# The second layer of a two-layer convolution kernel, written as a pipeline over half images

## The chip, the cores and the metric

The kernel runs on one core of a Trainium2 chip. The time is the device time of one execution of the whole program in microseconds (us), median over runs. The core has a matrix engine (TensorE, PE in the profile), VectorE (DVE), ScalarE (ACT), GpSimd (POOL) and SyncE (SP), which here only issues transfers (DMA). The engines run their own instruction streams and wait for one another through semaphores. ScalarE issues transfers too, from the same stream as its arithmetic: a transfer that waits there holds up the arithmetic behind it.

## The reference, cut to what matters

The input x is 32 images of 8 channels of 256 x 256, fp32. Each of two layers normalises x by groups of channels (`_gn`) and adds a function of the result to x. Layer 0 (a 15-step lattice, two small networks and a gate) is the greater part of the work and isn't touched. Layer 1 is a quantised 3 x 3 convolution:

```python
def _quantize(v, scale):
    return jnp.clip(jnp.round(v * scale), -MAX_Q, MAX_Q)
sx = MAX_Q / jnp.max(jnp.abs(x))          # over all 32 images
sw = MAX_Q / jnp.max(jnp.abs(weight))
qx = _quantize(x, sx)
qw = _quantize(weight, sw)
out_i32 = lax.conv_general_dilated(qx, qw, ...)   # 8 -> 8 channels, 3 x 3, padding 1
out = out_i32 / (sx * sw)
return out + bias[None, :, None, None]
...
x = x + _L1_conv_ref(_gn(x), L1_conv_weight, L1_conv_bias)
```

MAX_Q is 127. `sx` needs the largest value of all images, so layer 1 can't begin for any image before layer 0 has ended for all.

## The kernel before, in words

Layer 0 leaves its result y in HBM (`y_s`, one buffer per image, rows of 8 channels x 256 columns, with zero rows around them), and per image a mean `mean_y`, a factor `rstd_y` and a largest deviation `dev_y`. From line 898 on, layer 1 takes one image after the other.

An image is cut into 19 bands (`NB`) that step by 14 rows (`STEP`). Partition p of a band holds row p // 8 and channel p % 8, so 128 partitions are 16 rows of 8 channels: 14 output rows and a row of margin on each side. A tile of y is thus 128 x 19 x 256 fp32. The last band has 4 rows of output.

First come loads for three images, the largest deviation over partitions (a GpSimd all-reduce, L919) and small scale vectors (L921 to L929): `qs` has the scale, and two copies of it that zero the margin rows outside the image, for the first and the last band. Then, for each image b:

- VectorE subtracts the mean and scales, y to `tq` (L940 to L943, three instructions: band 0, bands 1 to 17, band 18).
- VectorE rounds `tq` to whole numbers in place, by adding and subtracting 1.5 x 2^23 (L944).
- VectorE clips to -127 and 127 and converts to bf16, `tq` to `qt` (L946). `qt` has a zero column on either side; there are two, taken in turn.
- TensorE runs over two bands at a time (512 columns), three matmuls for the three columns of the kernel, summed in a PSUM bank (L953). The rows and the channels are in the 128 x 128 weights `qw`.
- ScalarE scales each bank back, adds the bias and writes it to the output tile `ob` (L954); 10 such evictions make an image.
- ScalarE's queue issues the load of image b + 3 (L909), VectorE adds y to `ob` (L957), and SyncE issues 19 stores, one for each band, of 112 partitions x 1 KB (the last 32 partitions) to `out` (L960).

There are two `ob` tiles, four of y, one `tq` and four PSUM banks. An `ob` tile is free when all 19 stores have landed. The order on each engine around these lines is set by a scheduler, which takes the program's order as a priority and its own costs: ScalarE's queue issues the loads in pairs, and VectorE's sum of one image and scaling of the next change places in some images. Every transfer signals its landing on one of eight semaphores, taken in turn, and a transfer waits for the earlier one on the same semaphore, so that no more than eight are under way.

Of the kernel before, what the change touches and what calls it, by code (L numbers as in the profile page):

```python
# [31 lines left out]
F32 = mybir.dt.float32  # L32
BF16 = mybir.dt.bfloat16
F32R = mybir.dt.float32r
AF = mybir.ActivationFunctionType
ALU = mybir.AluOpType
AX = mybir.AxisListType
DRAM = bass.MemoryType.DRAM
PSUM = bass.MemoryType.PSUM

P = 128
C = 8
# [4 lines left out]
MAX_Q = 127.0  # L47
ROUND = 1.5 * 2.0**23

NB = 19  # L50
STEP = 14
PW = W + 2
# [61 lines left out]
def kernel(  # L114
# [15 lines left out]
    nc = tc.nc  # L130
    B = x.shape[0]
    V, S, G, T = nc.vector, nc.scalar, nc.gpsimd, nc.tensor

    def dram_ap(t, offset, dims):
        return bass.AP(t.tensor, t.offset + offset, dims)
# [17 lines left out]
    qw = cp.tile([P, 3, P], BF16, name="qw")  # L153
# [6 lines left out]
    mean_y = cp.tile([P, B], F32, name="mean_y")  # L160
# [96 lines left out]
    with ExitStack() as one:  # L257

        one.enter_context(tc.manual_schedule(engines={mybir.EngineType.PE}))
        pool = lambda name, bufs, **kw: one.enter_context(tc.tile_pool(name=name, bufs=bufs, **kw))  # L260
# [115 lines left out]
        def lattice(g):  # L376
# [77 lines left out]
            if g == 0:  # L454
                units[0], dmas = load(0)
                for d in dmas:
                    nc.sync.dma_start(*d)
                for ts in tiles:
                    begin(units[0], ts)
            for c in range(C):  # L460
                u = g * C + c
                ds = units[u]
                for step in range(STEPS):
                    if step == 7 and u + 1 < NG * C:
                        units[u + 1], dmas = load(u + 1)
                        later.extend(dmas)
# [363 lines left out]
        def chain(*gens):  # L830
            for gen in gens:
                yield from gen
# [15 lines left out]
        def both(a, t_a, b, t_b):  # L848

            done_a = done_b = 0.0  # L850
            while a or b:
                if b is None or a and done_a * t_b <= done_b * t_a:
                    w = next(a, None)
                    if w is None:
                        a = None
                        continue
                    done_a += w
                else:
                    w = next(b, None)
                    if w is None:  # L860
                        b = None
                        continue
                    done_b += w
                yield w

        def prep(g, halves):
            return normalise([(b, half) for half in halves for b in range(g * GB, g * GB + GB)])

        def images(f, g):
            for b in range(g * GB, g * GB + GB):  # L870
                yield from f(b)
# [3 lines left out]
        def after(g, gen):  # L875

            while issued[0] < stored[g]:
                yield 4.0
            yield from gen
# [3 lines left out]
        for g in range(NG):  # L883
            fill, t = images(nca, g), T_NCA
            if g:
                fill, t = both(fill, t, after(g - 1, images(gate, g - 1)), T_GATE), t + T_GATE
            if g + 1 < NG:
                fill, t = both(fill, t, prep(g + 1, (0, 1)), T_PREP), t + T_PREP
            if g == 0:
                fill, t = chain(prep(0, (1,)), fill), t + 20.0  # L890
# [7 lines left out]
    with ExitStack() as two:  # L898


        pool = lambda name, bufs, **kw: two.enter_context(
            tc.tile_pool(name=name, bufs=bufs, reuse_waits="tile", **kw)
        )
        tp, qp, op, sp, yp = pool("tp", 1), pool("qp", 2), pool("op", 2), pool("sp", 1), pool("yp", 4)
        ps = pool("ps", 4, space=PSUM)

        def load(b):
            y = yp.tile([P, NB, W], F32, name="yb", tag="yb")
            (nc.sync if b < 3 else nc.scalar).dma_start(  # L909
                y, dram_ap(y_s[b], 0, [[W, P], [STEP * C * W, NB], [1, W]])  # L910
            )
            return y

        ys = {b: load(b) for b in range(3)}

        gmax = sp.tile([P, 1], F32, name="gmax")
        V.tensor_reduce(gmax, dev_y, AX.X, ALU.max)
        gall = sp.tile([P, 1], F32, name="gall")
        G.partition_all_reduce(gall, gmax, P, bass.bass_isa.ReduceOp.max)  # L919
        sx = sp.tile([P, 1], F32, name="sx")  # L920
        V.reciprocal(sx, gall)  # L921
        V.tensor_scalar(sx, sx, MAX_Q, None, ALU.mult)
        inv = sp.tile([P, 1], F32, name="inv")
        V.tensor_tensor(inv, sx, sw, ALU.mult)
        V.reciprocal(inv, inv)
        qs = sp.tile([P, 3, B], F32, name="qs")
        V.tensor_scalar(qs[:, 0, :], rstd_y, sx, None, ALU.mult)
        V.tensor_scalar(qs[:, 1, :], qs[:, 0, :], masks[:, 2:3], None, ALU.mult)
        V.tensor_scalar(qs[:, 2, :], qs[:, 0, :], masks[:, 3:4], None, ALU.mult)  # L929
        qt = [qp.tile([P, NB, PW], BF16, name=f"qt{i}", tag=f"qt{i}", bufs=1) for i in range(2)]  # L930
        for t in qt:
            V.memset(t[:, :, 0], 0.0)
            V.memset(t[:, :, PW - 1], 0.0)

        for b in range(B):
            y = ys.pop(b)

            t = tp.tile([P, NB, W], F32, name="tq", tag="tq")
            for k0, k1, i in ((0, 1, 1), (1, NB - 1, 0), (NB - 1, NB, 2)):
                V.tensor_scalar(  # L940
                    t[:, k0:k1, :], y[:, k0:k1, :], mean_y[:, b : b + 1], qs[:, i, b : b + 1],
                    ALU.subtract, ALU.mult,
                )  # L943
            V.tensor_scalar(t, t, ROUND, ROUND, ALU.add, ALU.subtract)  # L944
            q = qt[b % 2]
            V.tensor_scalar(q[:, :, 1 : 1 + W], t, MAX_Q, -MAX_Q, ALU.min, ALU.max)  # L946
            o = op.tile([P, NB, W], F32, name="ob", tag="ob")
            for p in range(10):
                k0, n = 2 * p, (2 if p < 9 else 1)
                pt = ps.tile([P, 512], F32, name="pt2", tag="pt2")  # L950
                pt = pt[:, : n * W].rearrange("p (k w) -> p k w", w=W)
                for dx in range(3):
                    T.matmul(pt, qw[:, dx, :], q[:, k0 : k0 + n, dx : dx + W], start=(dx == 0), stop=(dx == 2))  # L953
                S.activation(o[:, k0 : k0 + n, :], pt, AF.Identity, bias=bv[:, 3:4], scale=inv)  # L954
            if b + 3 < B:
                ys[b + 3] = load(b + 3)
            V.tensor_tensor(o, o, y, ALU.add)  # L957
            for k in range(NB):
                rows = STEP if k < NB - 1 else 4
                nc.sync.dma_start(  # L960
                    dram_ap(out, b * C * H * W + STEP * k * W, [[W, rows], [H * W, C], [1, W]]),
                    o[C : C + rows * C, k, :],
                )


# [43 lines left out]
```

## Time and profile before

The time is 14360.28 us, the median of 3 runs (14354.44 to 14362.28). The profiled execution took 14414.7 us.

| what | value |
|---|---|
| span of the profiled execution | 14414.7 us |
| layer 0, up to the first load of y for layer 1 | 13636.3 us |
| layer 1, from there to the end | 778 us |
| 13700 to 14380 us: TensorE, VectorE, ScalarE, GpSimd busy | 244, 467, 199, 0 of 680 us |
| same: DMA engines' mean share, rate | 0.62, 189 GB/s |
| one load of y, one store of a band | 2432 KB, 112 KB |

Lines of the page with L940 to L960 belong to layer 1. In a row of a group, the numbers after `|` are busy us, mean ns of one instruction, the idle time just before the group's instructions and what ended most of it. In a row of waits, they are us in total, times, longest. In a table of stretches, each engine has busy us and the number of instructions, and the last three columns are the granted clock of TensorE as a share of the full one, the mean busy share of the 16 DMA engines and the rate. "ACTq" and "SPq" are the transfers that ScalarE and SyncE issue; the time that such a row gives is the issuing alone, not the transfer.

### The profile page before, as it was taken

How to read it: one execution, taken by the hardware profiler on the slowest of the kernel's cores; microseconds unless marked ns; L12 is line 12 of the kernel's file. 1: busy time of each engine (PE TensorE's matmuls, PEld its weight loads, DVE VectorE, ACT ScalarE, POOL GpSimd, SP SyncE). 2: the span in 40 equal slices, each digit the busy share in tenths (PEclk: the TensorE clock that was granted, in tenths of full speed). 3: DMA queues.
4: the chain of work that ended last, by engine and by line, in shares of the span. 5: the costliest groups of instructions: out<-in, count | busy, mean ns of one | idle time of the engine just before them, and what ended most of it. 6: DMA issues, size and time to landing. Idle time of an engine off the chain costs nothing.

```text
span 14414.7 us, 229163 instructions
## 1 busy us (share of the span) xinstructions
PE 13267.4 (92%) x81728; PEld 6423.3 (45%) x81728; DVE 8213.1 (57%) x16290; ACT 4039.8 (28%) x6274; POOL 2445.9 (17%) x4266
## 2 busy tenths in 40 slices
PE   2999999999999999999999999999999999999833
PEld 1554444444444444444444444444444444444311
DVE  3555555555555555555555555555555555555576
ACT  1333232232222222222322223222323222222122
POOL 1111111111111111111111111111111111112300
PEclk9999999999999999999999999999999999999966
DMA  5444444444444444444444434444444433333465
GB/s 148 93 97 92 90 103 106 103 94 100 110 94 100 99 106 94 103 100 95 100 103 107 98 93 106 110 94 94 104 104 98 103 88 88 80 83 78 122 195 176
DMA packets 2259559, 1496.74 MB, mean 104 GB/s; under 512 B 1061248, under 2 KB 2229504, under 8 KB 2258304
## 3 DMA queue, kind: packets, MB, share of 16 engines
q1 hardware_dynamic: 2176976, 1401.95, 41.9%
q10 hardware_dynamic: 81456, 80.12, 1.7%
q8 instruction: 664, 10.88, 0.3%
q14 instruction: 463, 3.79, 0.1%
HBM read 866.48 MB, written 478.69 MB: 93 GB/s over the span
## 4 chain that ended last, share of the span: by engine, by line
PE 70%; DMA 9%; DVE 9%; SPq 5%; issue 3%; POOL 2%; ACT 1%; ACTq 1%; POOLq 0%; DVEq 0%
PE pt L487 31%; PE ph L567 18%; PE pa L759 13%; PE acc L584 7%; DVE gt L495 2%; DMA im<-xp_s 1%; PE pg L725 1%; DMA xp_s<-lo 1%; SPq L545 1%; DVE m_b L500 1%; DMA xb<-in_x_dram 1%; DMA m_a<-m_a 1%; DMA out_dram<-ob 1%; SPq L960 1%; PE pt L953 1%
## 5 line engine op out<-in xcount | busy, mean ns | idle before, releaser
L487 PE MATMUL pt<-m_a,lw 128*64 128x390 f32 x17280 | 5827.0, 497 | 186.4 <-DMA m_a<-m_a 122.4
L487 PE MATMUL pt<-m_b,lw 128*64 128x384 f32 x17280 | 5796.6, 492 | 19.2 <-DVE m_b L410 18.0
L577 ACT ACTIVATE h<-ph,bp_sb 128x512 f32<-128x512 f32 x4096 | 2584.6, 684 | 6491.5 <-PE ph L567 6423.0
L487 PEld LDWEIGHTS pt<-m_a,lw 128*64 128x64 f32 x17280 | 2298.4, 138 | 1884.0 <-issue 1681.2
L487 PEld LDWEIGHTS pt<-m_b,lw 128*64 128x64 f32 x17280 | 2306.6, 138 | 1560.0 <-issue 1423.6
L567 PE MATMUL ph<-im,wp_hi 48*128 48x512 f32 x12288 | 2800.2, 419 | 174.2 <-DVE gt L495 113.1
L567 PE MATMUL ph<-im,wp_lo 48*128 48x512 f32 x12288 | 2675.2, 402 | 0.0
L495 DVE SCALAR_TENSOR_TENSOR gt<-pt,d_b 128x390 f32<-128x390 f32 x2880 | 1605.3, 557 | 1714.7 <-PE pt L487 1711.2
L495 DVE SCALAR_TENSOR_TENSOR gt<-pt,d_a 128x384 f32<-128x384 f32 x2880 | 1580.3, 549 | 1694.5 <-PE pt L487 1694.1
L504 POOL TENSOR_TENSOR m_b<-m_b,junk 128x12 f32<-128x12 f32 x2688 | 795.5, 296 | 8193.8 <-DVE m_b L500 7517.2
L567 PEld LDWEIGHTS ph<-im,wp_hi 48*128 48x128 f32 x12288 | 1417.5, 189 | 1081.7 <-DVE gt L495 303.9
L500 DVE SCALAR_TENSOR_TENSOR m_b<-gt 128x390 f32<-128x390 f32 x2688 | 1546.1, 575 | 44.5 <-DVE gt L495 2.3
L500 DVE SCALAR_TENSOR_TENSOR m_a<-gt 128x384 f32<-128x384 f32 x2688 | 1522.3, 566 | 17.2
L567 PEld LDWEIGHTS ph<-im,wp_lo 48*128 48x128 f32 x12288 | 1417.0, 189 | 217.3
L584 PE MATMUL acc<-h,wu_z 128*32 128x512 f32 x8320 | 1165.6, 603 | 6.1 <-ACT nca L602 5.5
L759 PE MATMUL pa<-xnb,gw 128*64 128x512 f32 (+1 forms) x3840 | 879.9, 588 | 43.7 <-DVE xnb L700 43.5
L759 PE MATMUL pa<-cmb,gw 128*64 128x512 f32 (+1 forms) x3840 | 857.6, 577 | 17.4 <-POOL cmb L681 17.4
L759 PE MATMUL pa<-nb,gw 128*64 128x512 f32 (+1 forms) x3840 | 863.6, 576 | 0.0
L730 POOL TENSOR_TENSOR d<-cmb,nb 128x512 f32<-128x512 f32 x320 | 502.9, 1572 | 1460.6 <-DVE gate L734 1028.5
L700 DVE TENSOR_SCALAR xnb<-xb,sc 128x256 f32<-128x256 f32 x608 | 290.7, 493 | 796.7 <-DMA xb<-in_x_dram 759.5
L953 PE MATMUL pt<-qt,qw 128*128 128x512 bf16 (+1 forms) x960 | 269.5, 451 | 477.0 <-ACT ob L954 425.4
L734 DVE TENSOR_TENSOR gate<-gate,d 128x512 f32<-128x512 f32 x320 | 217.4, 679 | 764.7 <-ACT gate L727 756.7
(132 smaller groups left out, 6928.0 us busy)
## 6 DMA issues: line engine op xcount, KB each, us to landing
im<-xp_s SPq DMA_DIRECT2D x1152, 193.5 KB
im<-xp_s SPq DMA_DIRECT2D x1216, 96.8 KB
d_a<-xq_s SPq DMA_DIRECT2D x2048, 36.0 KB
nb<-nc_s SPq DMA_DIRECT2D x288, 256.0 KB
cq<-cm_s SPq DMA_DIRECT2D x288, 256.0 KB
yb<-y_s ACTq DMA_DIRECT2D x29, 2432.0 KB
xb<-in_x_dram SPq DMA_DIRECT2D x544, 128.0 KB
xp_s<-hi SPq DMA_DIRECT2D x256, 258.0 KB
```

Of the source, the lines that this page charges most:

```text
L487: T.matmul(pt[half], lw[:, c, k, half], beside if part == 2 else own, start=part < 2, stop=part > 0,)
L495: V.scalar_tensor_tensor(gt, pt, FLOOR, d[:, ts, :], ALU.max, ALU.add)
L500: V.scalar_tensor_tensor(to, gt, 1.0, gt, ALU.subtract, ALU.mult)
L504: G.tensor_tensor(edge, edge, junk.unsqueeze(1).to_broadcast([P, 6, 2]), ALU.mult)
L567: T.matmul(ph[:, :n].rearrange("p (h w) -> p h w", w=W), w[64 * i : 64 * i + 48, dx, :], rhs[:, :, dx : dx + W], start=(dx == 0 and w is w ...
L577: S.activation(h[:, :n], ph[:, :n], AF.Relu, bias=bp_sb)
L584: T.matmul(acc[32 * g : 32 * g + 32, :cols], wu_z[:, 24 - 8 * i : 56 - 8 * i], h, start=first, stop=last,)
L700: V.tensor_scalar(xnb[:, k, 1 : 1 + W], xb[:, k, :], sc[:, i : i + 1], sc[:, 1:2], ALU.subtract, ALU.mult,)
L730: G.tensor_tensor(three(d), cmb[:, :n, 1 : 1 + W], nin, ALU.subtract)
L734: V.tensor_tensor(y[:, :cols], gt[:, :cols], d[:, :cols], ALU.mult)
L759: T.matmul(three[half], gw[:, s * 3 + dx, half], t[:, :n, dx : dx + W], start=(i == 0), stop=(i == 8),)
L953: T.matmul(pt, qw[:, dx, :], q[:, k0 : k0 + n, dx : dx + W], start=(dx == 0), stop=(dx == 2))
```

## The change

Layer 1 is written as a software pipeline whose order on all engines is that of the program (`manual_schedule`), with an image cut into halves of 10 and 9 bands. In iteration b VectorE scales image b in halves (`scaled`), rounding together with the lower clip: the rounding constant is added, then max with the constant minus 127. GpSimd does the rest (`quantised`): min with the constant plus 127, subtract the constant, convert to bf16. VectorE then adds y to the output of image b - 1, SyncE issues its first 13 stores, TensorE and ScalarE convolve image b and evict it, and behind these evictions ScalarE issues the other 6 stores of image b - 1 and the load of image b + 3. The zero columns are written by GpSimd, the first four loads are all on SyncE, and there are 8 PSUM banks, four `ob` and two `tq` tiles of half an image each. It is for having the engines work on different images at once, taking a pass from VectorE, and sharing the stores between two queues.

```diff
+        two.enter_context(tc.manual_schedule())
...
-        tp, qp, op, sp, yp = pool("tp", 1), pool("qp", 2), pool("op", 2), pool("sp", 1), pool("yp", 4)
-        ps = pool("ps", 4, space=PSUM)
+        tp, qp, op, sp, yp = pool("tp", 2), pool("qp", 1), pool("op", 4), pool("sp", 1), pool("yp", 4)
+        ps = pool("ps", 8, space=PSUM)
...
-            (nc.sync if b < 3 else nc.scalar).dma_start(
+            (nc.sync if b < 4 else nc.scalar).dma_start(
...
+        qt = [[qp.tile([P, n, PW], BF16, name=f"qt{i}{j}") for j, n in enumerate((10, 9))] for i in range(2)]
+        for t in (*qt[0], *qt[1]):
+            G.memset(t[:, :, 0], 0.0)
+            G.memset(t[:, :, PW - 1], 0.0)
+        HALVES = ((0, 10), (10, NB))
+        def scaled(b, y, h):
+            h0, h1 = HALVES[h]
+            t = tp.tile([P, 10, W], F32, name="tq", tag="tq")
             for k0, k1, i in ((0, 1, 1), (1, NB - 1, 0), (NB - 1, NB, 2)):
...
-            V.tensor_scalar(t, t, ROUND, ROUND, ALU.add, ALU.subtract)
-            q = qt[b % 2]
-            V.tensor_scalar(q[:, :, 1 : 1 + W], t, MAX_Q, -MAX_Q, ALU.min, ALU.max)
+            V.tensor_scalar(t, t, ROUND, ROUND - MAX_Q, ALU.add, ALU.max)
+            return t
+        def quantised(b, t, h):
+            G.tensor_scalar(qt[b % 2][h][:, :, 1 : 1 + W], t, ROUND + MAX_Q, ROUND, ALU.min, ALU.subtract)
...
+        last = None
+        for b in range(B + 1):
+            if b < B:
+                y = ys[b]
+                ts = [scaled(b, y, h) for h in range(2)]
+                for h in range(2):
+                    quantised(b, ts[h], h)
+            if last:
+                i, os_ = last
+                yi = ys.pop(i)
+                for h, (h0, h1) in enumerate(HALVES):
+                    o = os_[h][:, : h1 - h0, :]
+                    V.tensor_tensor(o, o, yi[:, h0:h1, :], ALU.add)
+                store(nc.sync, i, os_[0], 0, range(0, 10))
+                store(nc.sync, i, os_[1], 1, range(10, 13))
+            done = last
+            if b < B:
+                last = b, [convolved(b, h) for h in range(2)]
+            if done:
+                i, os_ = done
+                store(nc.scalar, i, os_[1], 1, range(13, NB))
+                if i + 4 < B:
+                    ys[i + 4] = load(i + 4)
```

## The prediction

> **What bounds the kernel now.** Only the second layer changes. It runs from the first load of y at 13636 us to the end at 14414.7 us, 778 us of the span, so I read views of that stretch alone. First the busy times of its steady part, columns length, busy time per engine, granted clock, DMA share, GB/s:
>
> ```profile
> 13700.00:14380.00 680.00, 244.26 (x873) 98.87 (x872) 467.05 (x171) 198.50 (x290) 0.00 (x0) 0.66 0.62 189
> ```
>
> No engine is full: VectorE (third) is at 69%, GpSimd at 0, DMA at 62%. So a wait sets the pace. The waits of the same stretch, all engines and then SyncE's queue:
>
> ```profile
> ACT ob L954 <- DMA out_dram<-ob: 446.8, 28, 26.4
> PE pt L953 <- ACT ob L954: 416.1, 29, 25.6
> DVE qt L946 <- PE pt L953: 121.0, 12, 10.7
> ...
> SPq L960 <- DMA yb<-y_s: 123.3, 25, 12.0
> SPq L960 <- DVE ob L957: 49.0, 12, 4.6
> ```
>
> ScalarE waits 447 of 680 us for an output tile to be stored, TensorE waits for ScalarE, VectorE for TensorE: everything queues behind the stores. Line L960 shows why, with L909 (the load) beside it; columns min/median/max ns:
>
> ```profile
> L960 SPq DMA_DIRECT2D out_dram<-ob x557: 652/817/1345, 13699.3 to 14379.3; - x186
> ...
> L909 ACTq DMA_DIRECT2D yb<-y_s x29: 366/366/395, 13637.5 to 14315.2; - x29
> ```
>
> One store holds the queue 0.82 us, 0.89 us from start to start in the trace. 19 stores make 16.9 us per image, then 123.3/28 = 4.4 us of waiting for a load and 1.8 us for the sum (L957): 23.1 us. Measured: L957 starts 48.1 us apart for each pair of images, **24.05 us per image**. The bound is one queue's issue plus its stalls.
>
> Work to be moved, by shape (busy us, mean ns):
>
> ```profile
> L946 DVE TENSOR_SCALAR qt<-tq 128x4864 bf16<-128x4864 f32 x29 | 151.4, 5222 | 122.6 <-PE pt L953 121.0
> L957 DVE TENSOR_TENSOR ob<-ob,yb 128x4864 f32<-128x4864 f32 x29 | 151.4, 5221 | 84.2 <-ACT ob L954 65.3 <-DMA out_dram<-ob 18.9
> ...
> L944 DVE TENSOR_SCALAR tq<-tq 128x4864 f32<-128x4864 f32 x29 | 78.1, 2694 | 1.0
> L940 DVE TENSOR_SCALAR tq<-yb,mean_y,qs 128x4352 f32<-128x4352 f32 x28 | 71.1, 2541 | 0.0
> L940 DVE TENSOR_SCALAR tq<-yb,mean_y,qs 128x256 f32<-128x256 f32 x56 | 22.9, 408 | 0.5
> L954 ACT ACTIVATE ob<-pt,bv,inv 128x256 f32<-128x256 f32 x29 | 16.4, 564 | 0.0
> ```
>
> The DMA ceiling shows where four loads run with nothing else:
>
> ```profile
> 13636.00:13668.00 32.00, 6.38 (x6) 0.51 0.98 312
> ```
>
> 98% busy at 312 GB/s. An image moves 2.49 MB in and 2.10 MB out, so **14.7 us per image** is the floor that no ordering passes.
>
> **What the Trainium skill says.** SBUF — State Buffer, § Who interferes with whom: VectorE in a 2-port mode, or with two SBUF inputs against a GpSimd read, and GpSimd exclude each other for a whole instruction. The trace agrees, in the first layer:
>
> ```profile
> 13566.38 1.27 POOL L730 TENSOR_TENSOR d<-cmb,nb 128x512 f32<-128x512 f32 x1 [10.56 <-DVE e L807]
> 13566.41 1.80 DVE L735 TENSOR_TENSOR gate<-gate,f 128x512 f32<-128x512 f32 x1
> ...
> 13576.44 0.69 DVE L735 TENSOR_TENSOR gate<-gate,f 128x512 f32<-128x512 f32 x1
> 13576.49 1.79 POOL L730 TENSOR_TENSOR d<-cmb,nb 128x512 f32<-128x512 f32 x1 [0.88 <-DVE gate L734]
> ```
>
> The same sum takes 0.69 us when it starts first and 1.80 us when GpSimd starts 0.03 us ahead. VectorE: DVE Perf Modes, § The perf-mode tier table: fp32 tensor_scalar runs at 2x, tensor_tensor at 1x; L944 (2694 ns) and L957 (5221 ns) for 4864 elements agree. So in the new order every VectorE instruction shuts GpSimd out. DMA: Bandwidth & Descriptors, § Issuing engines are not separate DMA queues: a second queue saves only issue time. That fits this trace, where issue time is what is short. GPSIMD Engine Reference, § 4.1, gives one-input work as "roughly line-rate"; no row of before is such an instruction.
>
> **The change part by part.**
> *Stores on two queues.* 13 of 19 stay on SyncE: 13 x 0.89 = 11.6 us, no longer the bound. 6 go behind ScalarE's ten evictions: 7.2 us (a full image in the trace takes 9 x 0.73 + 0.56) + 6 x 0.89 = 5.3 + load 0.4 = 12.9 us per image. I take a store's price on ScalarE as SyncE's, since loads cost 0.37 and 0.39 us on the two.
> *A new wait.* Transfers take eight semaphores in turn, and in the built program ScalarE's first store of an image waits for the load that ScalarE issued just before the evictions. The load lands 10.3 us after its issue with few stores beside it and 12.0 to 12.4 with ten (issue against last landing in the trace). Queued behind that wait are five stores, the next load and the next image's evictions. Cycle: landing 12.2 + six stores 5.3 + 0.1 = **17.6 us**; the evictions lie inside the landing. Ends: 10.3 gives 15.7, 13.0 gives 18.4.
> *VectorE.* The bf16 pass (5.22) leaves. Scaling in halves is 2 x 0.41 + 1.47 + 1.34, rounding with the lower clip 1.49 + 1.36, the sums 2.82 + 2.55 (times by elements from the rows above): 11.8 us.
> *GpSimd.* Two passes, 4864 elements, fp32 in, bf16 out. Not in the trace. Bounds:
>
> ```profile
> L732 POOL TENSOR_TENSOR f<-xb,nb 128x512 f32<-128x512 f32 x288 | 341.3, 1185 | 28.6 <-DVE gate L735 23.3 <-DMA nb<-nc_s 5.4
> L687 POOL MEMSET xb<- 128x512 f32 x64 | 34.6, 541 | 1.8
> L732 POOL TENSOR_TENSOR f<-xb,nb 128x256 f32<-128x256 f32 x32 | 21.5, 672 | 12.2 <-DVE gate L735 7.4 <-DMA cq<-cm_s 4.9
> ```
>
> Two inputs: (1185-672)/256 = 2.0 ns per element, 10.1 us with two starts. A pure write: (541-102)/510 = 0.86 (102 ns is the 2-element memset of L275), 4.4 us; line rate, by the skill. In between: the strided one-input copy (L681, 617 ns for 256 when undisturbed, 2.4 ns each), which GPSIMD Engine Reference, § 7 Performance pitfalls for Q7 kernels, puts 50% above an unstrided one: 1.6 ns, 7.8 us, an estimate. I take 6.5 us, between this and line rate, because the pass has no stride but two operations. It excludes VectorE, so the shared port needs 11.8 + 6.5 = **18.3 us**; ends 16.2 and 21.9.
> *At nothing:* loads from bf16 halves and 8 PSUM banks (TensorE needs 8.2 us per image, less than any bound above); four output halves (same SBUF); border zeros on GpSimd (0.1 us each, while VectorE scales image 0); the fourth load on SyncE (needed only by image 3). GpSimd's reload after the all-reduce is up to 10 us, under the first scaling of 6.4 us and VectorE's scaling of image 1, which waits for its load (13660.6): a few us once, not counted.
>
> *The sum.* Period 18.3, taken as 18.4 for two nearly equal loops. First sum as before at 13677; 31 periods are 570.4; then half a sum 2.8, 13 stores 11.6, landing 2.4 and the 3.0 between the last landing and the end in the trace before: 14267, against 14414.7. Saving 147 us, and 14360.3 - 147 = **14213 us**. For another period P: 14213 + 31 x (P - 18.4).
>
> **Rivals.**
> *GpSimd at the two-input price.* P = 21.9: 14322 us. For it: L732; against it: one input is read, not two.
> *GpSimd at line rate and a quick landing.* P = 16.2, with the load landing in under 11 us: 14145 us. For it: 10.3 us landings exist; against: those loads had three stores beside them, and 13 or more will now fly.
> *ScalarE in series, slower.* ScalarE takes things in order. If GpSimd, held off by back-to-back VectorE instructions, delivers the second half only when the load has landed, evictions no longer lie inside the landing: 12.2 + 7.2 + 5.3 = 24.7, 14408 us. For it: the long in-order chain; against: VectorE and GpSimd work an image ahead of ScalarE, through four bf16 tiles.
>
> **How the numbers follow.** Forecast (P from 17.3 to 20) 0.62, first rival 0.20, second 0.12, third 0.06. Range 14140 (P 16.0) to 14310 (P 21.5), which leaves the third, the top of the first and little else outside. No change within 0.2% (29 us) needs P between 22.2 and 24: 0.03; slower 0.05; faster 0.92.
>
> **What would show it.** Right: sums 18 to 19 us apart; ScalarE's queue waiting for the load of y, no longer evictions for stores; VectorE's instructions stretched by GpSimd; VectorE plus GpSimd filling the period; DMA share about 0.8. Wrong: GpSimd passes far from 3.4 us each, VectorE at its old durations beside a busy GpSimd, stores on ScalarE far from 0.89 us apart, or a load landing beyond 14 us.

## The result, and the profile after

The changed kernel takes 14465.06 us (median of 4 runs, 14460.20 to 14468.12), the kernel before beside it 14357.36 us: a ratio of 1.0075, 95% interval 1.0057 to 1.0092. It is slower by 108 us, where 147 us less were forecast. The time is in layer 1: from the first load of y to the end it takes 893 us (13568.8 to 14461.9), before 778 us. (The profiled execution of before spent 67 us longer in layer 0, on the same instructions, so the two spans can't be subtracted.)

The steady stretch, in the same columns as before:

```profile
13700.00:14380.00 680.00, 270.39 (x758) 99.14 (x758) 678.25 (x203) 182.86 (x252) 506.19 (x52) 0.66 0.59 171
```

VectorE went from 467 to 678 of 680 us: by its record it never rests. GpSimd is at 506. The DMA share fell from 0.62 to 0.59, and the forecast had it at 0.8. The waits of all engines from 13750 to 14400 us:

```profile
...
ACT ob L967 <- PE pt L963: 472.8, 160, 11.1
PE pt L963 <- POOL qt L953: 391.2, 48, 10.5
POOL qt L953 <- DVE tq L949: 139.4, 43, 5.2
```

and of SyncE's queue:

```profile
SPq L973 <- DVE ob L992: 368.7, 48, 14.8
```

Nobody waits for a store or a load any more. ScalarE waits for TensorE, TensorE for GpSimd, and SyncE's stores for VectorE's sum. The groups of the two engines at the head of this queue, by shape:

```profile
L953 POOL TENSOR_SCALAR qt<-tq 128x2304 bf16<-128x2304 f32 x24 | 249.0, 10376 | 41.3 <-DVE tq L949 41.3
...
L944 DVE TENSOR_SCALAR tq<-yb,mean_y,qs 128x256 f32<-128x256 f32 x49 | 232.2, 4739 | 0.0
L992 DVE TENSOR_TENSOR ob<-ob,yb 128x2304 f32<-128x2304 f32 x24 | 231.5, 9645 | 0.0
...
L992 DVE TENSOR_TENSOR ob<-ob,yb 128x2560 f32<-128x2560 f32 x24 | 67.6, 2818 | 0.0
L949 DVE TENSOR_SCALAR tq<-tq 128x2560 f32<-128x2560 f32 x24 | 35.8, 1494 | 0.8
...
L949 DVE TENSOR_SCALAR tq<-tq 128x2304 f32<-128x2304 f32 x24 | 32.6, 1359 | 0.8
```

One sum of 2560 elements takes 2.8 us and the smaller one of 2304 takes 9.6; a scaling of 256 elements has a mean of 4.7 us, against 0.41 before. No work explains that: these are the instructions that start while GpSimd is in a pass. The timeline of one image shows it:

```profile
14015.77 10.16 DVE L944 TENSOR_SCALAR tq<-yb,mean_y,qs 128x2048 f32<-128x2048 f32 x2
...
14016.03 9.75 POOL L953 TENSOR_SCALAR qt<-tq 128x2560 bf16<-128x2560 f32 x1 [5.16 <-DVE tq L949]
...
14025.97 1.36 DVE L949 TENSOR_SCALAR tq<-tq 128x2304 f32<-128x2304 f32 x1
14027.24 12.38 DVE L992 TENSOR_TENSOR ob<-ob,yb 128x2560 f32<-128x2560 f32 x2
14027.51 10.38 POOL L953 TENSOR_SCALAR qt<-tq 128x2304 bf16<-128x2304 f32 x1 [1.72 <-DVE tq L949]
```

The two scalings of the second half (1.34 and 0.41 us of work) last 10.16 us, as long as GpSimd's pass beside them; two sums (2.8 and 2.5) last 12.38 us around the second pass. The bars overlap, the work doesn't: the engine that came second waits. Less what it waited for the instruction ahead, GpSimd holds the port for about 8.7 us (10 bands) and 7.8 us (9 bands), **16.5 us per image, 3.4 ns per element**. The passes of image 0, which find VectorE idle, take nearly the same, 8.87 and 7.95 us. The first sums of successive images (VectorE's sum for the first half image, one per image) start 27.01 us apart, to 0.01 us. In the first version below, whose loop runs through a load, these distances vary from 16.6 to 18.4 us (from 13750 us on).

### The profile page after: what moved, and what is told of

The parts are those of the page before. It is cut to its first block, busy times and chain, and to the rows that moved or that the text cites. A ratio compares the mean times of both kernels' runs of the same rounds, so it can differ in the third digit from the quotient of the medians.

```text
span 14461.9 us, 229407 instructions
## 1 busy us (share of the span) xinstructions
PE 13323.7 (92%) x81728; PEld 6437.2 (45%) x81728; DVE 8550.3 (59%) x16350; ACT 4058.2 (28%) x6274; POOL 3092.8 (21%) x4338
## 4 chain that ended last, share of the span: by engine, by line
PE 71%; DVE 13%; DMA 6%; SPq 4%; issue 3%; POOL 1%; ACTq 1%; ACT 1%; POOLq 0%; DVEq 0%
PE pt L487 31%; PE ph L567 18%; PE pa L759 13%; PE acc L584 7%; DVE tq L944 3%; DVE ob L992 3%; DVE gt L495 2%; DMA im<-xp_s 1%; PE pg L725 1%; DMA xp_s<-lo 1%; SPq L545 1%; DVE m_b L500 1%; DMA xb<-in_x_dram 1%; DMA m_a<-m_a 1%; DVE m_a L500 1%
## 5 line engine op out<-in xcount | busy, mean ns | idle before, releaser
L487 PE MATMUL pt<-m_b,lw 128*64 128x384 f32 x17280 | 5787.6, 491 | 19.1 <-DVE m_b L410 17.7
L500 DVE SCALAR_TENSOR_TENSOR m_a<-gt 128x384 f32<-128x384 f32 x2688 | 1528.6, 569 | 17.2
L963 PE MATMUL pt<-qt,qw 128*128 128x512 bf16 (+1 forms) x960 | 343.5, 537 | 533.9 <-POOL qt L953 533.9
L953 POOL TENSOR_SCALAR qt<-tq 128x2560 bf16<-128x2560 f32 x64 | 640.9, 10014 | 219.5 <-DVE tq L949 183.3
```

What stands on the lines that cost most here:

```text
L487: T.matmul(pt[half], lw[:, c, k, half], beside if part == 2 else own, start=part < 2, stop=part > 0,)
L500: V.scalar_tensor_tensor(to, gt, 1.0, gt, ALU.subtract, ALU.mult)
L953: G.tensor_scalar(qt[b % 2][h][:, :, 1 : 1 + W], t, ROUND + MAX_Q, ROUND, ALU.min, ALU.subtract)
```

## The experiments

The theory that these views give: the port that VectorE and GpSimd share carries VectorE's 11.8 us and GpSimd's 16.5 us one after the other, 28.3 us less some overlap at the ends of the instructions, which is to make the 27.0 us measured; and the forecast failed by the price of GpSimd's pass alone. Rivals: the stores on two queues, or the new order, make the period; or the pass is dear only because VectorE keeps breaking in. The first versions were timed on a chip on which the kernel before took 14361 us, the later ones, from the half pass on, on three others (14399 to 14404 us), so ratios to the kernel before are compared. The times expected were worked out for the chip of the result above; "on the first chip's scale" is the ratio times its 14357 us.

**The pass given back to VectorE.**

```diff
-  G.tensor_scalar(qt[b % 2][h][:, :, 1 : 1 + W], t, ROUND + MAX_Q, ROUND, ALU.min, ALU.subtract)
+  V.tensor_scalar(qt[b % 2][h][:, :, 1 : 1 + W], t, ROUND + MAX_Q, ROUND, ALU.min, ALU.subtract)
```

> One part undone: the clip and conversion go back to VectorE, everything else as changed. Theory (the period is VectorE plus GpSimd on one port, 27.0 us): without GpSimd VectorE needs 11.8 + 5.3 = 17.1 us, the store and load loop of ScalarE 15.1 (load landing 9.7 us, six stores 5.3), DMA 14.7: period 17.2, and 14465 - 31 x (27.0 - 17.2) = 14161 us. Rival (the in-order streams, the six stores on ScalarE or the semaphores hold it, GpSimd's time being hidden): 14430 us or more.

14157.89 us, ratio 0.9856 (0.9841 to 0.9870). All the rest of the change together is a gain of 1.4% (its parts aren't taken one by one); the pass on GpSimd costs 2.2% (0.9856 to 1.0075) and turns it into a loss. The time expected came out, but not by the term that was to set it: the first five distances between sums are 15.28 us, with VectorE never idle in them, so VectorE needs 15.3 us and not 17.1. The later distances, 17.1 us on the average, come from ScalarE's loop through a load (70.5% of the chain of waits from 13800 to 14050 us is that load), which is read further down.

**All stores on SyncE**, GpSimd's pass kept.

```diff
-  store(nc.scalar, i, os_[1], 1, range(13, NB))
+  store(nc.sync, i, os_[1], 1, range(13, NB))
```

> One part undone: all 19 stores on SyncE, the GpSimd pass as changed. Theory: SyncE then needs 16.9 us of 27.0, so nothing moves but the tail, where six stores more come after one another, 5 us: 14465 to 14475 us, sums still 27.0 us apart. Rival (ScalarE's stores hold the evictions up): the period falls by up to 5.3 us, 14300 to 14400 us.

14490.08 us, ratio 1.0088 (1.0071 to 1.0105), an interval that overlaps that of the changed kernel; the sums are still 27.01 us apart. Sharing the stores between two queues plays no part in the loss. The time is some 10 us above the one expected, and the tail is where they are: from the start of the last image's first sum to the end it takes 27.5 us instead of 17.2, where 5 us more were expected.

**Each form by itself.** Both layers are left out; the instructions run on constant data, 2560 elements per partition, four times, with the other engine idle.

> Leaves both layers out: the same GpSimd instruction by itself, nine forms of it four times each on 2560 elements, with VectorE idle, then four forms on VectorE. Theory (the GpSimd pass costs 3.4 ns per element of its own, whatever VectorE does): the form of the changed kernel, two operations, bf16 out with a padded row, takes 8.6 to 8.8 us here too. Rival 1 (the pass is stretched by VectorE's instructions): it takes 2.2 to 5.2 us here. Rival 2 (the bf16 output, or its padded and shifted rows, make it dear): the fp32 form or the form without padding takes 5 us or less, the padded one 8.7. Rival 3 (the second operation): the one-operation forms take half. On VectorE: 2560 fp32 to fp32 1.49 us; the padded bf16 form 2.8 us if the shift by one element forbids the quick mode, 1.5 if only an odd number of rows did.

Groups by shape. L150, L151 and L152 are the pass of the change (min, subtract) to the padded bf16 tile, to plain bf16 and to fp32; L153 and L155 a subtraction alone; L156 and L157 copies to bf16 and fp32; L158 a sum of two tiles; L161 and L162 VectorE's own pass to the padded bf16 tile, with 10 and with 9 rows:

```profile
L150 POOL TENSOR_SCALAR qp<-t 128x2560 bf16<-128x2560 f32 x4 | 35.3, 8825 | 3.2 <-DVE t L145 3.2
...
L152 POOL TENSOR_SCALAR v<-t 128x2560 f32<-128x2560 f32 x4 | 35.2, 8812 | 0.0
...
L155 POOL TENSOR_SCALAR v<-t 128x2560 f32<-128x2560 f32 x4 | 26.7, 6667 | 0.0
...
L158 POOL TENSOR_TENSOR v<-t,u 128x2560 f32<-128x2560 f32 x4 | 22.3, 5570 | 0.3
L162 DVE TENSOR_SCALAR qp<-t 128x2304 bf16<-128x2304 f32 x4 | 10.2, 2557 | 0.1
...
L156 POOL CAST qp<-t 128x2560 bf16<-128x2560 f32 x4 | 9.3, 2318 | 0.0
L161 DVE TENSOR_SCALAR qp<-t 128x2560 bf16<-128x2560 f32 x4 | 6.0, 1489 | 0.0
```

Undisturbed, the pass takes 8.82 us, so VectorE doesn't make it dear, and neither do bf16 or the padding. The second operation doesn't either: the subtraction alone takes 6.67 us, three quarters of it and not half. The pass costs more than a sum of two tiles (5.57), which the forecast had held to be the dearest it could be. On VectorE, 10 rows take 1.49 us and 9 rows 2.56 (1.11 ns per element). So the shifted column isn't what makes such a pass slow. The bf16 pass of before (19 rows, 5.22 us, 1.07 ns) has the price of an odd number of rows; 19 rows weren't timed in another way. The Trainium skill has a rule that fits, in VectorE: DVE Perf Modes, § What auto-detection actually checks: a single source runs in the two-port mode when the outermost dimensions of source and destination are both even or equal. The 9 rows of the padded tile stand against a source without gaps. The two times agree with the rule if such a source counts as one row of 2304, which no run here tests.

**VectorE's pass in even bands.** The 9 bands of the second half are taken as 8 and 1.

```diff
+  n = t.shape[1] // 2 * 2
+  for a, z in ((0, n), (n, t.shape[1])):
+      if a < z:
+          V.tensor_scalar(qt[b % 2][h][:, a:z, 1 : 1 + W], t[:, a:z, :], ROUND + MAX_Q, ROUND, ALU.min, ALU.subtract)
```

> As the first experiment, but the second half's pass is cut into 8 bands and 1, so that each piece but the last has an even number of rows. If only the odd number of rows kept VectorE's bf16 pass from its quick mode, it costs 1.5 + 1.25 + 0.3 us instead of 5.3, VectorE 14.9 us, and the period is 15.1 to 15.6, set by ScalarE's loop and DMA: 14465 - 31 x (27.0 - 15.4) = 14105 us. If the shift by one element forbids the mode, the period is 17.5, 14170 us, no better than the first experiment.

14147.71 us, ratio 0.9854 (0.9839 to 0.9869), where 14105 us were expected: the even bands are quick (8 and 1 bands take 1.22 and 0.29 us, and the first four distances between sums are 14.16 us), but the time is that of the odd bands. What holds it is the chain of waits from 13800 to 14050 us, by line:

```profile
by line: DMA yb<-y_s 70.6%; ACTq L978 27.8%; issue 2.6%
```

and ScalarE in the timeline:

```profile
13920.05 0.46 ACTq L910 DMA_DIRECT2D yb<-y_s  x1
...
13920.71 6.58 ACT L972 ACTIVATE ob<-pt,bv,inv 128x512 f32<-128x512 f32 x10 [10.47 <-DMA out_dram<-ob]
...
13931.70 5.47 ACTq L978 DMA_DIRECT2D out_dram<-ob  x6
...
13937.21 0.46 ACTq L910 DMA_DIRECT2D yb<-y_s  x1
```

The load is issued, the evictions are done at 13927, the first store starts at 13931.7 when the load has landed, six stores follow, and the next load 17.16 us after the last. This is the wait that the forecast described (landing 12.2 + stores 5.3 + 0.1 = 17.6); measured here are 11.6 + 5.5.

**Half of the pass on each engine** (first half image VectorE, second GpSimd).

```diff
-  G.tensor_scalar(qt[b % 2][h][:, :, 1 : 1 + W], t, ROUND + MAX_Q, ROUND, ...)
+  (V if h == 0 else G).tensor_scalar(qt[b % 2][h][:, :, 1 : 1 + W], t, ROUND + MAX_Q, ROUND, ...)
```

> The clip and conversion of the first half image (10 bands) is done by VectorE, that of the second (9 bands) stays on GpSimd. Theory (one port, GpSimd's pass at 3.44 ns per element): VectorE 11.0 + 1.5 us, GpSimd 7.9 us, together 20.4 us per image between sums instead of 27.0, so 14465 - 31 x 6.6 = 14260 us. Rival (the pass on GpSimd costs a fixed time per image through its place in the order, not by its elements): sums still 24 us apart or more, 14370 us or more.

Ratio 0.9928 (0.9914 to 0.9943), 14254 us on the first chip's scale; sums 19.91 us apart (20.4 expected). The rule of the sum holds between the two ends.

**GpSimd only converts**; VectorE does the min and the subtraction in fp32.

```diff
-  G.tensor_scalar(qt[b % 2][h][:, :, 1 : 1 + W], t, ROUND + MAX_Q, ROUND, ALU.min, ALU.subtract)
+  V.tensor_scalar(t, t, ROUND + MAX_Q, ROUND, ALU.min, ALU.subtract)
+  G.tensor_copy(qt[b % 2][h][:, :, 1 : 1 + W], t)
```

> Minimum and subtraction are done by VectorE in fp32, in place, at its 2x rate (1.49 + 1.36 us); GpSimd only copies the result into the bf16 tile (2.3 + 2.1 us by the rate of the run that timed each form by itself). Theory: VectorE 11.0 + 2.9, GpSimd 4.4, together 18.3 us per image, near the forecast's 18.4, so 14465 - 31 x 8.7 = 14195 us: GpSimd can have a pass, but not an arithmetic one. Rival (any pass on GpSimd in this place costs much the same, by waits between the two engines): 24 us per image or more, 14370 us or more.

Ratio 0.9883 (0.9868 to 0.9897), 14189 us on that scale; sums 18.11 us apart, though two instructions more were issued than in the change. A pass on GpSimd isn't dear by itself.

**The kernel before, with its clip and conversion on GpSimd**, and nothing else of the change.

```diff
-  V.tensor_scalar(q[:, :, 1 : 1 + W], t, MAX_Q, -MAX_Q, ALU.min, ALU.max)
+  G.tensor_scalar(q[:, :, 1 : 1 + W], t, MAX_Q, -MAX_Q, ALU.min, ALU.max)
```

> The kernel before with one part of the change alone: the clip and conversion (line 946) is moved to GpSimd, everything else is as before. Theory: VectorE's scaling, rounding and sum 11.3 us and GpSimd's pass 4864 x 3.44 = 16.7 us exclude each other, 28 us per image against 24.05, so 14357 + 31 x 4 = 14480 us (14460 to 14545, by how the scheduler places them). Rival, the forecast's price (6.5 us): 17.8 us of port time hide under the stores' 23 to 24 us, 14330 to 14360 us.

Ratio 0.9991 (0.9984 to 0.9998), no loss, where 14480 us were expected. The theory fell here, by its price: groups by shape,

```profile
L957 DVE TENSOR_TENSOR ob<-ob,yb 128x4864 f32<-128x4864 f32 x28 | 188.7, 6738 | 230.2 <-ACT ob L954 159.2 <-DMA out_dram<-ob 71.0
...
L946 POOL TENSOR_SCALAR qt<-tq 128x4864 bf16<-128x4864 f32 x26 | 110.3, 4242 | 484.9 <-DVE tq L944 259.8 <-PE pt L953 225.2
```

4864 elements take GpSimd 4.24 us, not 16.7: **0.87 ns per element**, for the same kind of instruction and the same types as in the change. What differs is the two operations, min with max here and min with subtract there, and with them the constants and the size of the tile. VectorE's sum still waits for it (6.74 us against 5.22), so the port is shared as before, but 4.2 us hide in a kernel that its stores bound.

**The operations one by one**, set up as for the forms above, on constant data.

> Both layers are left out; GpSimd does 2560 elements per partition in one form after the other, with VectorE idle. In the version that moved the old clip alone, min with max took 4.24 us for 4864 elements, 0.87 ns each. Theory (the operations decide): min, and min with max, at about 0.87 ns, 2.3 us, whatever the constants; every form with an addition, subtraction or multiplication at 6.7 us (one) or 8.8 us (two, or one with a min or max), as min with subtract was measured. Rival (subtraction alone is slow): add and mult near 2.3 us as well. Rival (the size of the constants or of the tile decides): min with max at 1.5 x 2^23 is slow too, or min with max at 127 is slow here.

The lines of that kernel, with what each does:

```
L150, L151: min 127, max -127 (to bf16, to fp32)   L156: add, max
L152: min alone                                    L157: add alone
L153: min, max with constants of 1.5 x 2^23        L158: multiply alone
L154: min, subtract (the change)                   L159: multiply, add
L155: add, subtract                                L160, L161: sum, product of two tiles
```

```profile
L155 POOL TENSOR_SCALAR v<-t 128x2560 f32<-128x2560 f32 x4 | 35.3, 8829 | 0.3
L156 POOL TENSOR_SCALAR v<-t 128x2560 f32<-128x2560 f32 x4 | 35.3, 8817 | 0.3
L154 POOL TENSOR_SCALAR v<-t 128x2560 f32<-128x2560 f32 x4 | 35.3, 8817 | 0.3
L158 POOL TENSOR_SCALAR v<-t 128x2560 f32<-128x2560 f32 x4 | 26.7, 6676 | 0.3
...
L152 POOL TENSOR_SCALAR v<-t 128x2560 f32<-128x2560 f32 x4 | 26.6, 6659 | 0.3
...
L150 POOL TENSOR_SCALAR qp<-t 128x2560 bf16<-128x2560 f32 x4 | 9.3, 2322 | 3.2 <-DVE t L145 3.2
L159 POOL TENSOR_SCALAR v<-t 128x2560 f32<-128x2560 f32 x4 | 9.3, 2324 | 0.3
L153 POOL TENSOR_SCALAR v<-t 128x2560 f32<-128x2560 f32 x4 | 9.3, 2320 | 0.3
```

The theory holds in part: min with max is quick with either set of constants, and add, subtract or multiply cost what was expected, but for one pair. Neither rival holds. Arithmetic isn't slow as such: multiply with add takes 2.32 us. Min isn't quick as such: alone it takes 6.66. Two *pairs* are quick, min with max and multiply with add (this one tried with one set of constants); every other form with constants that was tried takes 6.7 us with one operation and 8.8 with two. With a max or an add as second operation, a min or a multiplication thus becomes 2.9 times shorter. Why just these two are quick isn't shown.

**The same four operations, shared out the other way.**

```diff
-  V.tensor_scalar(t, t, ROUND, ROUND - MAX_Q, ALU.add, ALU.max)
+  V.tensor_scalar(t, t, ROUND, ROUND, ALU.add, ALU.subtract)
...
-  G.tensor_scalar(qt[b % 2][h][:, :, 1 : 1 + W], t, ROUND + MAX_Q, ROUND, ALU.min, ALU.subtract)
+  G.tensor_scalar(qt[b % 2][h][:, :, 1 : 1 + W], t, MAX_Q, -MAX_Q, ALU.min, ALU.max)
```

> The changed kernel with the four operations shared out the other way, in as many instructions: VectorE rounds (add, subtract the constant), GpSimd clips (min 127, max -127) and converts to bf16. Theory: GpSimd's passes take 2.3 + 2.0 us instead of 8.7 + 7.8, so the port needs 11.1 + 4.3 = 15.4 us per image, below ScalarE's loop of load landing and six stores (17.1): 17.1 us between sums and 14465 - 31 x 9.9 = 14158 us, ratio 0.986, about where VectorE doing all of it ended (0.985). Rival (GpSimd's 16.5 us came from its place in this order): 24 us or more, 14370 us or more.

Ratio 0.9852 (0.9837 to 0.9867), 14145 us on the first chip's scale. In the groups by shape GpSimd's passes are now

```profile
L953 POOL TENSOR_SCALAR qt<-tq 128x2560 bf16<-128x2560 f32 x25 | 81.3, 3253 | 250.3 <-DVE tq L949 250.3
...
L953 POOL TENSOR_SCALAR qt<-tq 128x2304 bf16<-128x2304 f32 x25 | 52.8, 2110 | 43.1 <-DVE tq L949 37.9 <-PE pt L963 5.2
```

with no instruction added, moved or taken away, and VectorE's rounding at 1.49 us for 10 bands as in the change. The first four distances between sums are 15.33 us, where 15.4 were put for both engines on the port; the later ones are 17.1 us on the average, by ScalarE's loop again (70.5% of the chain from 13800 to 14050 us is the load, 27.8% its stores). So the loss came from which two of four operations were given to GpSimd.

**Three tries at the loop that is left.** First, loads issued by GpSimd, on top of the version with even bands:

```diff
-  (nc.sync if b < 4 else nc.scalar).dma_start(
+  (nc.sync if b < 4 else nc.gpsimd).dma_start(
```

> The version in which VectorE clips and converts in even bands (14148 us, 16.8 us per image), and the loads of images 4 to 31 are issued by GpSimd instead of ScalarE. Theory: the 16.8 us are ScalarE's loop of the load's landing (11.7) and six stores (5.3); with the load off that queue the loop opens and the next bound is VectorE's 14.1 us or the transfers' 14.7 us, so about 15.3 us per image and 14148 - 31 x 1.5 = 14100 us. Rival: GpSimd's issue of a load is itself held up by VectorE, or the transfers already set the 16.8 us: 14140 us or more.

Ratio 0.9834 (0.9818 to 0.9851), 14119 us on the first chip's scale. That lies between the theory and its rival. Half of the sums are now 14.85 us apart: VectorE's 14.16 us, and 0.65 more in the instruction that starts beside GpSimd's issue of a load. Others are up to 21.5 us apart, the mean from the 6th to the 30th distance is 16.2. It has the lowest ratio of all, but its interval overlaps those of the versions with 0.985. It isn't shown to be faster than they are, only than the two kernels of this study. Then three stores moved from ScalarE to SyncE, on top of the shared-out version:

```diff
-  store(nc.sync, i, os_[1], 1, range(10, 13))
+  store(nc.sync, i, os_[1], 1, range(10, 16))
...
-  store(nc.scalar, i, os_[1], 1, range(13, NB))
+  store(nc.scalar, i, os_[1], 1, range(16, NB))
```

> The version before this one (VectorE rounds, GpSimd clips with min and max) with 16 of the stores on SyncE and 3 on ScalarE, instead of 13 and 6. Theory: ScalarE's loop shrinks by three stores, 17.1 - 2.7 = 14.4 us; SyncE needs 16 x 0.89 = 14.2; the port's 15.4 us become the bound: 15.5 us per image, 14465 - 31 x 11.5 = 14108 us, ratio 0.983, so 0.003 below the 13 and 6 split. Rival (the stores' and the load's transfers set 17 us, not the loop): no gain over the 13 and 6 split, 14150 us or more.

Ratio 0.9895 (0.9879 to 0.9912), worse by 0.4%. The chain from 13800 to 14050 us shows a loop, but another one:

```profile
by line: DMA yb<-y_s 73.1%; SPq L973 18.5%; DMA out_dram<-ob 13.8%; issue 1.8%
```

With another count, the semaphores fall on other transfers: SyncE's stores wait for the load, and the next load for their landing; loads are issued 17.8 to 19.8 us apart. The rival that transfers set 17 us is no better off, since 17.1 became 18.3 with the same bytes. Last, six output tiles instead of four, on top of the version with GpSimd's loads:

```diff
-  pool("op", 4)
+  pool("op", 6)
```

> The version with the loads on GpSimd's queue and the clip in even bands on VectorE (ratio 0.983 to the kernel before, sums 14.85 to 18 us apart, mean about 16.3), with six half-image output tiles instead of four. Theory: what held it above VectorE's 14.85 us was ScalarE in series, because the evictions of a second half reuse the tile whose stores ScalarE has only just issued: 7.2 evictions + 5.3 stores + about 4 landing = 16.5 us. With two more tiles these evictions need a tile of one image earlier, the landing leaves the loop, and VectorE sets about 15 us: 14465 - 31 x 12 = 14093 us on the chip of the first runs, ratio 0.9815. Rival (the transfers themselves set about 16.3 us, 0.86 of the DMA engines' time): no gain, ratio 0.983 or more.

Ratio 0.9855 (0.9835 to 0.9875): no gain, and the theory of ScalarE in series falls. The sums are 14.85 to 25.5 us apart, and the chain from 13800 to 14050 us is

```profile
by line: DMA out_dram<-ob 55.6%; SPq L978 18.2%; ACT ob L972 14.4%; ACTq L978 5.5%; issue 3.3%; DVE ob L997 2.6%; DVE tq L944 0.7%; DVE qt L956 0.1%
```

Stores that land 2.5 us after their issue in most cases when no load runs take up to 11.8 us beside one (from 13750 to 14180 us a quarter of this version's stores take over 8.7 us), and the stores behind them on the same semaphores wait. Whether more semaphores or a steadier mixture would bring 15 us wasn't tried.

## Why the prediction was wrong

**The bound before, right as far as it is shown.** The trace before has everything queued behind the stores, and without GpSimd's pass the rest of the change gains 1.4 to 1.5%. No run moves stores to a second queue and leaves all else as before, so this bound is read from waits, not tested alone.

**The exclusive port, right.** VectorE and GpSimd add up. By the sum, VectorE's 11.85 us and the passes alone (8.82 us, and nine tenths of it for 9 bands: 7.94) make 28.6 us; measured are 27.01. With half the pass it is 11.85 + 1.49 + 7.94 = 21.3 against 19.91, with GpSimd's copies 11.85 + 2.84 + 4.41 = 19.1 against 18.11. The instructions' ends overlap a little, 1.0 to 1.6 us per image. Of this 0.6 to 0.7 us lie between VectorE's own instructions: with the pass on VectorE, in odd and in even bands, its instructions add up to 15.90 and 14.85 us, and the first distances are 15.28 and 14.16.

**The price of GpSimd's pass, wrong, and the step that failed.** The forecast took 6.5 us, between 4.4 and 10.1 as ends; it is 16.5. The first of its signs of being wrong came true, passes far from 3.4 us each (8.7 and 7.8). The estimate was high for an instruction with a quick pair (4.2) and 2.5 times too low for this one. Its upper end came from the sum of two tiles (L732), on the thought that one input can't cost more than two. The forms by themselves refute it: 3.4 ns per element against 2.2. The one instruction with one input that the trace had, the strided copy at 2.4 ns, was brought down to 1.6 for its stride, and the 6.5 us taken (1.3 ns) lie below even that, with two operations added. Measured, a plain copy takes 0.9 ns, so the 1.6 was off as well, and the choice of operations decides. The Trainium skill's sentence that one-input work is "roughly line-rate" (GPSIMD Engine Reference, § 4.1) pulled the same way; it holds here for copies, min with max and multiply with add (0.9 ns), not for the other pairs or for one operation.

With this term put right alone, P is 28.6 and the forecast's own formula gives 14213 + 31 x 10.2 = 14529 us; with the measured P = 27.0 it gives 14213 + 31 x 8.6 = 14480 us. So this one term is large enough for the miss of 252 us, and the overlap of the ends takes a part back. That 14480 comes within 15 us of the measurement is in part luck: the first sum comes 53.3 us after the first load and not 41.0 as before, as GpSimd's first two passes stand ahead of it, but the last distance is 12.3 us and not 27.0, and the tail after it 17.2 and not 19.8.

Three readings in the working are off too, by little: the pairs of sums before are 47.8 us apart on the average (23.9 us per image, not 24.05), TensorE needs 8.6 us per image (244.26 us in 680), not 8.2, and from the last landing to the end it is 0.9 us, not 3.0.

**The range and the chances, wrong with it.** The formula reaches the time before, 14360, at P = 18.4 + 147 / 31 = 23.1 us, that is when GpSimd takes more than 11.3 us. The trace had no instruction of this kind on GpSimd, so nothing bounded it there, and 0.05 for slower rested on an unsound end. The rival that was slower, ScalarE in series, isn't what happened: after the change ScalarE waits for TensorE, and the load lands in 9.7 us without anybody waiting for it.

**Stores and the new wait, right but hidden.** Stores on ScalarE are 0.90 us apart on the average, as on SyncE. The loop of landing and six stores was put at 17.6 us, and is 17.1 us where GpSimd's pass doesn't hide it. There it is longer than what the port carries (15.3 us with min and max on GpSimd). At the forecast's own price the port's 18.3 us would have stayed the longer of the two, as it did with GpSimd's copies (18.1 us).

## What to carry to other kernels

An instruction of a kind that the trace doesn't hold has no upper bound from its neighbours: work out at which price the verdict turns, and measure that form by itself before it goes into a loop. On GpSimd choose the pair of operations, not only the engine: when four operations have to be split between two engines, the split that gives GpSimd min with max, multiply with add or a plain copy was up to 3.8 times cheaper there (2.32 us against 8.82), and what GpSimd takes is also taken from a VectorE whose instructions share its port. VectorE at nearly 100%, with times that jump between equal instructions (0.41 and 8.9 us), was waiting inside its instructions; that wait is in no table of waits.

## What was not expected of the hardware

- GpSimd on 2560 fp32 elements per partition: copy, cast, min with max, multiply with add 2.32 us; sum or product of two tiles 5.57; one operation with a constant 6.66 to 6.68; the other pairs 8.81 to 8.83. Type and padding of the output changed nothing in the forms tried.
- Four loads alone moved 312 GB/s at 0.98 of the DMA engines' time, and the version with GpSimd's loads moved 280 at 0.86, which is 326 at the full share. The same division gives 305 for the kernel before and 323 with six tiles, so 326 is no sure figure. By it, as an estimate, the 4.59 MB of an image take 14.1 us, so that the forecast's 14.7 is no hard floor. The lowest mean distance of sums was 16.2 us, and no run comes near enough to tell.
- A load of 2432 KB costs GpSimd 2.24 us to issue, against 0.37 to 0.46 us on ScalarE, and a VectorE instruction that starts beside it is drawn out (2.14 us instead of 1.49).
